# Order of GpSimd's and VectorE's first instructions in a four-layer position-dependent convolution network

## The chip, the cores and the metric

The kernel runs on one core of one Trainium2 chip. The metric is the device time of one execution in microseconds (us), taken as the median over the executions that were timed. A profiled execution is a separate one, and its trace gives start and duration of the instructions of each engine: PE (TensorE matmul, with PEld for its weight loads), DVE (VectorE), ACT (ScalarE), POOL (GpSimd) and SP (SyncE, which here only starts transfers).

## The reference

Four layers, each added to its input: x = x + layer(group_norm(x)), with x of shape (4, 32, 32, 16). Layers 0, 1 and 3 are of one kind, and nearly all of the time goes into them. Cut to what matters:

```
def conv(inputs, M, W, G):            # inputs: batch 4, 32 x 32, 16 channels
    first = einsum('ijyx,byxc->bijc', M, inputs)
    kern = G as (1024*16, 16, 3, 3)   # a 3x3 kernel for each of 1024 output places, 16 channels
    shifted = conv2d(inputs, kern, padding='SAME')       # 16384 images of 32 x 32 for each batch element
    diff = relu(inputs[:, None, None] - shifted)
    second = einsum('ijyx,bijyxc->bijc', W, diff)
    return first - second
```

Layer 2 is a small network of running maxima and 16-wide products; the change does not touch it.

## The kernel before

**Tiling.** The batch of four is done as two groups of two images, and the three large layers times two groups give six phases (`conv_layer`). A phase has 8 chunks of 128 output places. A chunk is 32 steps, one for each of 16 channels f and two images b. A step is one [128 x 1024] result in PSUM (`pc`), made by matmuls over the nine taps (eight taps as two times 64 rows on each half, the ninth on its own), and then one VectorE instruction (line 728, tile `junk`) which takes min(result, 0), multiplies it by the weights `WT` and adds up along the row. There are 1536 steps. The PSUM pool has four buffers of that size, so the first matmul of step k can start when the line 728 instruction of step k-4 has read its buffer.

**Weights and units.** Weights come in units of four channels. Units 0 and 1 of the first chunk (`PLAIN = 2`) are used as they are, in float32: tile `first`, with the ninth tap's weights in `W9`. Their steps are the first 16 and in this order: channels 0 to 3 of image 0, channels 0 to 3 of image 1, then channels 4 to 7 of both in the same way. This text numbers them 0 to 15. Step 16 is the first of unit 2. From unit 2 on, both operands are split into a high and a low part, and the products are taken in a faster format: `ib` and `ia` hold the images' parts in other partitions and `iyz` a difference of parts.

**Preparation of a unit.** From unit 2 on, the generator `prep_parts` prepares units: VectorE cuts off low bits (line 206, tile `upper_w`), ScalarE and GpSimd make `parts` and `W9` (lines 178 and 242 to 251), SyncE copies parts to other partitions (line 257) and loads a later unit (line 111). Ahead of this, GpSimd subtracts one from one tap's weights (`minus_center`, line 220), for unit 2 and later in `raw`, for the plain units in `first`. `prep_plain` and `prep_plain_rest` make a plain unit's `W9` (line 178 on ScalarE, then line 181 on VectorE).

**The first images.** The images of the first phase come by transfer in three slots into `raw`. `sides` sets the edges of the shifted copies (lines 915 and 922), `normal` applies mean and inverse deviation (lines 929, 930 and 932), `halve` and `halve_rest` make the ninth tap's image `im9`.

**Split, place, difference.** For units 2 and later each image is split: `split` has VectorE cut the image (line 206, tile `upper_x`) and subtract (line 289, two instructions, one for each slot s), and ScalarE scale the upper part (line 293). Both write into `temp`, which lies in `first` behind the plain weights. `place` has SyncE copy from `temp` into `ib` (line 305, four transfers) and `ia` (line 311, four transfers). `difference` (line 297, one instruction for each s) makes `iyz` on VectorE from `temp`. A write of the second image's part of `temp` by line 289 waits for two of the first image's `ia` transfers, the second and the fourth, since the ranges that they read reach into it.

**What sets the order.** Each engine runs its instructions in the order in which the program issues them. `conv_layer` issues one step at a time; between steps it takes the next piece of the generators `prep_parts` and `behind`. A `yield 1` of `behind` puts the following piece behind the next step, `yield 2` behind the one after that. In the first phase `behind` runs `rest_of_start` first, where two of the three edits are; the other stands in the straight code before it. In the order of issue, a step's matmuls of its first part come ahead of the line 728 instruction of the step before.

Of the kernel before, what the change touches and what calls it, by code (L numbers as in the profile page):

```python
# [18 lines left out]
GB = B // NG  # L19
# [26 lines left out]
def net_kernel(ctx: ExitStack, tc: tile.TileContext, x, xq, xi, convs, iv_w, iv_b, out):  # L46
# [26 lines left out]
    nc = tc.nc  # L73
# [33 lines left out]
    def load_raw(u):  # L107
        if u < n_chunks * NU:
            n = u // NU
            raws[u] = wpool.tile([P, 3, FU, P], F32, tag="raw", bufs=RAWS, name=f"raw_{u}")  # L110
            nc.sync.dma_start(raws[u], convs[phases[n // NT][1]][2][n % NT, u % NU])
# [65 lines left out]
    def halve(dst, src, mask):  # L177
        nc.scalar.activation(dst, src, AF.Copy, scale=mask[:, 1:2])  # L178

    def halve_rest(dst, src, mask):  # L180
        nc.vector.scalar_tensor_tensor(  # L181
            dst, src, mask[:, 0:1], dst.bitcast(F32), op0=ALU.mult, op1=ALU.add
        )
# [5 lines left out]
    def zeros(g):  # L189

        nc.gpsimd.memset(xt[g], 0.0)
        for y in (0, HP - 1):
            nc.gpsimd.dma_start(
                xs[g][:, :, y * WP : (y + 1) * WP], zero[:GC].rearrange("p (h n) -> p h n", h=2)
            )
# [3 lines left out]
    def image(v, x):  # L199
        return v.rearrange("... (y x) -> ... y x", x=x)[..., :HW]  # L200
# [10 lines left out]
    def prep(u, at=0, to=FU, eng=nc.gpsimd):  # L211

        if u >= n_chunks * NU:
            return
        for s in range(2 if u < PLAIN else 1):
            minus_center(eng, u, s, at, to)

    def minus_center(eng, u, s, at, to):
        f0 = u % NU * FU
        eng.tensor_tensor(  # L220
            raws[u][:, s, at:to], raws[u][:, s, at:to],
            pick[s][:, f0 + at : f0 + to].unsqueeze(2).to_broadcast([P, to - at, P]),
            ALU.subtract,
        )
# [46 lines left out]
    def prep_plain(u, at=0, to=FU, eng=nc.gpsimd):  # L271
        plain_unit(u)
        prep(u, at, to, eng)
        halve(units[u][3][:, at:to], raws[u][:, 2, at:to], low_p)

    def prep_plain_rest(u, at=0, to=FU):
        halve_rest(units[u][3][:, at:to], raws[u][:, 2, at:to], low_p)

    def halves(temp, b):
        v = temp[:, :TEMP].rearrange("p (k s b n) -> p k s b n", k=2, s=2, b=GB)  # L280
        return v[:, 0, :, b], v[:, 1, :, b]

    def split(eng, g, b, temp, name, pause=IDLE):

        ty, tz = halves(temp, b)
        high = upper(image(raw[:, :2, b], WP), 2, f"x{name}{b}")
        yield 1
        for s in range(2):
            eng.tensor_tensor(
                image(tz[:, s], HW), image(raw[:, s, b], WP), image(high[:, s], HW), ALU.subtract  # L290
            )
            yield pause
            nc.scalar.activation(ty[:, s], high[:, s], AF.Copy, scale=EPS)  # L293

    def difference(eng, g, b, s, temp):
        ty, tz = (v.bitcast(F32)[:, s] for v in halves(temp, b))
        eng.tensor_tensor(iyz[g][:, s, b], ty, tz, ALU.subtract)

    def place(g, b, temp):

        parts = halves(temp.bitcast(F32)[:, :TEMP], b)
        da, db = (v[g].bitcast(F32)[:, :, b] for v in (ia, ib))
        for lo, hi in QUARTERS:
            for to, src in zip((lo, hi), parts):
                nc.sync.dma_start(db[to], src[hi])
        for h, (lo, hi) in enumerate(QUARTERS):
            for k, to in enumerate((lo, hi)):
                at = (2 * k * GB + b) * NH + HW * (1 - h)
                pitch = GB * NH + HW * (2 * h - 1)
                src = temp.bitcast(F32)[lo, at : at + 2 * pitch].rearrange("p (s n) -> p s n", s=2)  # L310
                nc.sync.dma_start(da[to, :, :LAST], src[:, :, :LAST])
        yield 1
# [468 lines left out]
    def behind(phase):  # L781
        g, layer = phases[phase]
        if phase == 0:
            yield from rest_of_start()
            nc.sync.dma_start(X[1], x[1])
            zeros(1)
            yield 6
            yield from constants()
        if phase + 1 < len(phases):
            g1, layer1 = phases[phase + 1]  # L790
            if layer1 == 2:
                yield from interval_layer(g1)
            terms = g1 == NG - 1 and layer1 < NL - 1
            yield from before_conv(g1, layer1)
            if terms:
                mt = yield from load_first_terms(layer1)
                yield from first_terms(layer1, mt)
        if phase == len(phases) - 1:
            mt = yield from load_first_terms(layer)
            yield from first_terms(layer, mt)  # L800
            yield 4
            nc.sync.dma_start(out[1 - g], X[1 - g])
# [107 lines left out]
    def sides(eng, b, slot, only=("left", "right", "top", "bottom")):  # L910

        v = raw[:, slot, b].rearrange("p (y x) -> p y x", x=WP)
        if slot == 2:
            at = v[64:, :, HW - 1]
            eng.tensor_scalar(at, at, mean0[64:, b : b + 1], None, op0=ALU.add)
        for side, at in (
            ("left", v[:, :, 0]), ("right", v[:, :, HW - 1]),
            ("top", v[:, 0, :HW]), ("bottom", v[:, H - 1, :HW]),
        ):
            if side in only and f"{side}{slot}" in keep:  # L920
                k = keep[f"{side}{slot}"]
                eng.tensor_scalar(  # L922
                    at, at, kept[:, k : k + 1], fill[:, b, k : k + 1], op0=ALU.mult, op1=ALU.add
                )

    def normal(eng, b, slot):
        v = raw[:, slot, b, :RUN]
        if eng is nc.scalar:
            eng.activation(v, v, AF.Identity, bias=minus_mean0[:, b : b + 1])
            eng.activation(v, v, AF.Copy, scale=rstd0[:, b : b + 1])  # L930
        else:
            eng.tensor_scalar(  # L932
                v, v, mean0[:, b : b + 1], rstd0[:, b : b + 1], op0=ALU.subtract, op1=ALU.mult
            )

    sides(nc.vector, 0, 0)
    sides(nc.gpsimd, 0, 2)
    minus_center(nc.gpsimd, 0, 1, 0, F0)
    sides(nc.gpsimd, 0, 1, ("left", "right"))
    nc.vector.reciprocal(rstd0, rstd0)  # L940
    normal(nc.scalar, 0, 2)
    normal(nc.vector, 0, 0)
# [7 lines left out]
    def rest_of_start():  # L950

        nc.sync.dma_start(X[0], x[0])
        load_raw(2)
        load_raw(3)
        prep_plain_rest(0, F0, FU)
        yield 1
        sides(nc.gpsimd, 1, 2)
        sides(nc.gpsimd, 1, 1, ("left", "right"))
        sides(nc.vector, 1, 0)
        sides(nc.vector, 1, 1, ("top", "bottom"))  # L960
        for eng, slot in ((nc.scalar, 2), (nc.vector, 0), (nc.vector, 1)):
            normal(eng, 1, slot)
        halve(image(im9[0][:, 1], HW), image(raw[:, 2, 1], WP), low_x)
        halve_rest(image(im9[0][:, 1], HW), image(raw[:, 2, 1], WP), low_x)
        prep_plain(1)
        prep(2)
        yield 1
        prep_plain_rest(1)
        yield 1
        temp = first.bitcast(F32R)[:, used:]  # L970
        for b in range(GB):
            yield from split(nc.vector, 0, b, temp, "00", 1)
            yield from place(0, b, temp)
            for s in range(2):
                difference(nc.vector, 0, b, s, temp)
            yield 1
        nc.gpsimd.memset(zero, 0.0)
        nc.vector.memset(part, 0.0)
        zeros(0)
        xns[0] = work.tile([P, NT, GC], F32, tag="xn", bufs=2, name="xn_00")  # L980
        yield from group_norm(0, "c00", xns[0], 4, CALM)
# [83 lines left out]
```

## Time and profile before

| | us |
|---|---|
| median of 3 runs | 2467.36 |
| lowest and highest run | 2466.83, 2468.67 |
| the profiled execution | 2469.47 |
| its span, from first to last instruction | 2467.4 |
| PE busy in the span | 2457.5 |
| DVE busy | 2075.6 |
| POOL busy | 1594.7 |
| PE busy from 0 to 52 us | 47.8 |
| PE busy from 52 to 100 us | 48.0 |
| PE busy from 100 to 400 us | 299.9 |
| PE busy from 400 to 2400 us | 1998.8 |

The last four rows are read from a table of busy time by stretches of the span. PE is busy nearly everywhere behind 52 us. Time in which PE has nothing to do lies ahead of 52 us, where the change is made, and at the very end. The granted TensorE clock is 1.00 in each of these stretches.

### The profile page before, as it was taken

To read this page: it belongs to the slowest core of one execution; us is meant where nothing else is said; L and a number is where in the kernel's file an instruction comes from. 1 tells how busy PE (TensorE), PEld (TensorE's weight loads), DVE (VectorE), ACT (ScalarE), POOL (GpSimd) and SP (SyncE) were. 2 spreads that over 40 slices of the span, in tenths; PEclk is the share of its full clock that TensorE was granted. 3 is DMA by queue.
4 is the path that set the end of the run, shared out by engine and by line. 5 is a ranking of instruction groups with operands and counts; after the bars stand their busy time and mean duration, and the time that the engine had idled before them with its cause. 6 is when DMAs were issued, how large, how long until landed. Compare 5 with 4: busy or idle time off the path is not lost.

```text
span 2467.4 us, 58148 instructions
## 1 busy us (share of the span) xinstructions
PE 2457.5 (100%) x21928; PEld 2056.1 (83%) x21928; DVE 2075.6 (84%) x3631; ACT 1873.6 (76%) x2164; POOL 1594.7 (65%) x1864
## 2 busy tenths in 40 slices
PE   9999999999999999999999999999999999999999
PEld 5888888888888888888888888888889888888887
DVE  9888878888888888878898888888888888788887
ACT  4777777787777778767777777777777787677776
POOL 5767665676666667555576876776777675555552
PEclk9999999999999999999999999999999999999999
DMA  7456654485444467644554454664444476554452
GB/s 202 138 156 162 185 179 137 127 200 141 133 143 135 137 168 186 199 113 137 138 139 131 126 142 136 168 179 137 128 136 136 128 206 179 147 148 137 138 137 55
DMA packets 96906, 366.92 MB, mean 149 GB/s; under 512 B 25712, under 2 KB 30704, under 8 KB 96624
## 3 DMA queue, kind: packets, MB, share of 16 engines
q1 hardware_dynamic: 96064, 362.79, 53.4%
q8 instruction: 172, 2.82, 0.5%
q14 instruction: 110, 0.90, 0.1%
q10 hardware_dynamic: 432, 0.39, 0.1%
q0 software_dynamic: 128, 0.02, 0.0%
HBM read 199.78 MB, written 1.02 MB: 81 GB/s over the span
## 4 chain that ended last, share of the span: by engine, by line
PE 96%; DVE 1%; DMA 1%; ACT 1%; issue 1%; POOL 0%; ACTq 0%; DVEq 0%; POOLq 0%
PE pc L675 95%; PE pf L451 1%; DVE junk L728 1%; DMA raw<-in_g 0%; ACT pc L711 0%; DMA first<-in_g 0%; ACT temp L293 0%; PE ps_l L585 0%; DMA ib<-first 0%; PE ps_r L600 0%; DVE raw L922 0%; DVE im L181 0%; DVE W L181 0%; DVE raw L932 0%; ACT im L178 0%
## 5 line engine op out<-in xcount | busy, mean ns | idle before, releaser
L728 DVE SCALAR_TENSOR_TENSOR junk<-pc,WT 128x1024 f32<-128x1024 f32 x1536 | 1879.3, 1224 | 354.4 <-PE pc L675 295.2
L711 ACT ACTIVATE pc<-pc 128x1024 f32<-128x1024 f32 x1520 | 1532.2, 1008 | 560.5 <-PE pc L675 525.2
L675 PE MATMUL pc<-iyz,parts 64*128 64x512 f32 x6080 | 943.3, 387 | 2.1 <-ACT pc L711 1.6
L675 PE MATMUL pc<-ib,parts 64*128 64x512 f32 x6080 | 945.2, 387 | 0.2
L675 PE MATMUL pc<-ia,parts 64*128 64x496 f32 x6080 | 920.8, 379 | 0.0
L675 PEld LDWEIGHTS pc<-ia,parts 64*128 64x128 f32 x6080 | 578.8, 184 | 111.7
L675 PEld LDWEIGHTS pc<-ib,parts 64*128 64x128 f32 x6080 | 576.9, 184 | 108.4 <-issue 5.0
L675 PEld LDWEIGHTS pc<-iyz,parts 64*128 64x128 f32 x6080 | 577.3, 184 | 97.9 <-ACT pc L711 7.3
L675 PE MATMUL pc<-im,W 64*128 64x496 f32 x3072 | 598.6, 383 | 0.0
L243 POOL TENSOR_TENSOR parts<-raw,upper_w 128x512 fp32r<-128x512 f32 x190 | 249.5, 1313 | 522.7 <-DVE upper_w L206 440.9
L675 PEld LDWEIGHTS pc<-im,W 64*128 64x128 f32 x3072 | 292.7, 184 | 59.9 <-issue 3.3
L249 POOL CAST parts<-parts 32x512 fp32r<-32x512 f32 x380 | 231.7, 610 | 36.0 <-ACT parts L246 17.4
L247 POOL TENSOR_TENSOR parts<-parts 128x512 fp32r<-128x512 f32 x190 | 247.5, 1303 | 1.6 <-ACT parts L242 1.5
L244 POOL TENSOR_TENSOR W<-W,raw 128x512 fp32r<-128x512 f32 x190 | 247.8, 1304 | 0.3 <-ACT W L178 0.3
L251 POOL CAST parts<-upper_w 32x512 fp32r<-32x512 f32 x380 | 233.1, 613 | 22.8
L220 POOL TENSOR_TENSOR raw<-raw,ident 128x512 f32<-128x512 f32 x190 | 197.9, 1042 | 59.3 <-DMA raw<-in_g 35.4
L178 ACT ACTIVATE W<-raw,low_w 128x512 fp32r<-128x512 f32 x190 | 136.2, 717 | 3.7 <-DMA raw<-in_g 3.7
L728 DVE DVE_READ_ACCUMULATOR junk<-pc,WT 128x1 f32 x1536 | 127.6, 83 | 0.0
L242 ACT ACTIVATE parts<-upper_w 128x512 fp32r<-128x512 f32 x190 | 118.7, 624 | 3.8 <-DVE upper_w L206 3.7
L246 ACT CAST parts<-upper_w 128x512 fp32r<-128x512 f32 x190 | 116.1, 611 | 0.0
L743 POOL TENSOR_SCALAR acc<-acc 128x32 f32<-128x32 f32 x40 | 15.7, 392 | 133.9 <-DVE junk L728 132.1
L206 DVE TENSOR_SCALAR upper_w<-raw 128x512 int32<-128x512 int32 x190 | 82.1, 432 | 10.2 <-POOL raw L220 9.9
(158 smaller groups left out, 481.2 us busy)
## 6 DMA issues: line engine op xcount, KB each, us to landing
raw<-in_g SPq DMA_DIRECT2D x190, 768.0 KB, 7.2
parts<-parts SPq DMA_DIRECT2D x380, 384.0 KB, 5.0
WT<-in_w SPq DMA_DIRECT2D x48, 512.0 KB, 4.8
MT<-in_mt SPq DMA_DIRECT2D x24, 512.0 KB, 7.5
raw<-xs SPq DMA_DIRECT2D x120, 71.8 KB, 3.5
ib<-temp SPq DMA_DIRECT2D x40, 128.0 KB, 7.4
ia<-temp SPq DMA_DIRECT2D x40, 124.0 KB, 6.0
ib<-first SPq DMA_DIRECT2D x8, 128.0 KB, 4.0
```

The source lines that it names most:

```text
L178: nc.scalar.activation(dst, src, AF.Copy, scale=mask[:, 1:2])
L220: eng.tensor_tensor(raws[u][:, s, at:to], raws[u][:, s, at:to], pick[s][:, f0 + at : f0 + to].unsqueeze(2).to_broadcast([P, to - at, P]), ...
L242: nc.scalar.activation(WD, high, AF.Copy, scale=-EPS)
L243: nc.gpsimd.tensor_tensor(WL, w8, high, ALU.subtract)
L244: nc.gpsimd.tensor_tensor(W9, W9.bitcast(F32), src[:, 2], ALU.add)
L246: nc.scalar.copy(WU, high)
L247: nc.gpsimd.tensor_tensor(WD, WD.bitcast(F32), WL.bitcast(F32), ALU.add)
L249: nc.gpsimd.tensor_copy(WU[hi], WL[lo].bitcast(F32))
L251: nc.gpsimd.tensor_copy(WL[lo], high[hi])
L675: nc.tensor.matmul(ps[:, h, at : at + n], lhsT=w[r], rhs=v[r] if n == NH else v[r][:, :n], start=first and k == 0, stop=k == len(pairs) - ...
L711: nc.scalar.activation(ps, ps, AF.Copy, scale=1.0 + EPS)
L728: nc.vector.scalar_tensor_tensor(junk, ps.rearrange("p h n -> p (h n)"), 0.0, chunks[n], op0=ALU.min, op1=ALU.mult, accum_out=accs[phase][ ...
```

## The change

```diff
     sides(nc.vector, 0, 0)
     sides(nc.gpsimd, 0, 2)
+    sides(nc.gpsimd, 0, 1, ("left", "right"))
     minus_center(nc.gpsimd, 0, 1, 0, F0)
-    sides(nc.gpsimd, 0, 1, ("left", "right"))
     nc.vector.reciprocal(rstd0, rstd0)
...
         prep_plain(1)
         prep(2)
-        yield 1
+        yield 2
         prep_plain_rest(1)
-        yield 1
         temp = first.bitcast(F32R)[:, used:]
         for b in range(GB):
             yield from split(nc.vector, 0, b, temp, "00", 1)
             yield from place(0, b, temp)
+        for b in range(GB):
             for s in range(2):
                 difference(nc.vector, 0, b, s, temp)
             yield 1
```

No instruction is added or removed; some change places.

- On GpSimd, the two edge instructions (line 922) of slot 1 of image 0 come ahead of the subtraction (line 220) of the second half of unit 0's first two channels.
- On VectorE, the instruction that completes unit 1's `W9` (line 181) stood between the line 728 instructions of steps 1 and 2, ahead of `upper_w` of unit 2 (line 206). It now stands behind the line 728 instruction of step 2, ahead of `upper_x` of image 0. `upper_w` of unit 2 thereby comes directly behind the line 728 instruction of step 1.
- On VectorE, the two line 297 instructions of image 0 stood ahead of image 1's `upper_x` and line 289 instructions. They now stand behind them: between the line 728 instructions of steps 10 and 11, and those of image 1 follow between steps 11 and 12, where they were. Image 1's `upper_x` comes one step earlier than before (ahead of the line 728 instruction of step 7), and so do its two line 289 instructions (ahead of those of steps 8 and 9).
- ScalarE's and SyncE's instructions keep their order, and so do all that follow step 12.

## The prediction

> **What bounds the kernel now.** I read the chain that ended last for the whole span, then only its first 100 us in order of time, then the timelines of PE, DVE, POOL and SP there, and the transfers' landings. Over the span PE is the chain:
>
> ```profile
> PE 96%; DVE 1%; DMA 1%; ACT 1%; issue 1%; POOL 0%; ACTq 0%; DVEq 0%; POOLq 0%
> ```
>
> Behind 52 us PE idles 1.7 us in all, so what PE loses or gains ahead of that goes to the end one for one. Ahead of it DVE sets PE's pace. DVE's timeline (start, us; line; what), with the lines that matter:
>
> ```profile
> 19.34 1.53 DVE L181 SCALAR_TENSOR_TENSOR W<-first,low_p,W 128x512 fp32r<-128x512 f32 x1
> 20.79 0.41 DVE L206 TENSOR_SCALAR upper_w<-raw 128x512 int32<-128x512 int32 x1
> 21.13 1.21 DVE L728 SCALAR_TENSOR_TENSOR junk<-pc,WT 128x1024 f32<-128x1024 f32 x1
> ...
> 22.27 0.84 DVE L206 TENSOR_SCALAR upper_x<-raw 128x1024 int32<-128x1024 int32 x1
> 23.03 1.21 DVE L728 SCALAR_TENSOR_TENSOR junk<-pc,WT 128x1024 f32<-128x1024 f32 x1
> ...
> 28.99 2.13 DVE L297 TENSOR_TENSOR iyz<-first 128x512 fp32r<-128x512 f32 x2
> 31.05 1.21 DVE L728 SCALAR_TENSOR_TENSOR junk<-pc,WT 128x1024 f32<-128x1024 f32 x1
> ...
> 33.94 0.68 DVE L289 TENSOR_TENSOR first<-raw,upper_x 128x512 fp32r<-128x512 f32 x1
> ...
> 39.09 1.35 DVE L297 TENSOR_TENSOR iyz<-first 128x512 fp32r<-128x512 f32 x2
> ```
>
> It has no gap worth naming from 9.9 to 52 us. PE follows it through the four PSUM buffers: step 6 starts at 22.40, when step 2's line 728 (21.13 + 1.21 = 22.34) is done, and step 17 at 43.27, when that of step 13 (42.00 to 43.22) is.
>
> ```profile
> 22.40 1.99 PE L675 MATMUL pc<-raw,first 64*128 64x512 f32 x8 [0.63 <-DVE junk L728]
> ```
>
> GpSimd's timeline:
>
> ```profile
> 16.67 1.06 POOL L220 TENSOR_TENSOR first<-first,ident 128x512 f32<-128x512 f32 x1 [0.16 <-DMA first<-in_g]
> 19.28 1.04 POOL L220 TENSOR_TENSOR raw<-raw,ident 128x512 f32<-128x512 f32 x1 [1.55 <-DMA raw<-in_g]
> 21.28 1.28 POOL L243 TENSOR_TENSOR parts<-raw,upper_w 128x512 fp32r<-128x512 f32 x1 [0.96 <-DVE upper_w L206]
> ...
> 29.15 1.43 POOL L220 TENSOR_TENSOR raw<-raw,ident 128x512 f32<-128x512 f32 x1
> ...
> 39.67 1.28 POOL L193 DMA_DIRECT2D xs<-zero  x2
> 40.93 1.32 POOL L247 TENSOR_TENSOR parts<-parts 128x512 fp32r<-128x512 f32 x1
> ```
>
> Beside DVE's lines these show a shared resource. Line 297 alone takes 0.68; the second of the pair at 28.99 took 1.53 and ended at 31.13, 0.55 behind GpSimd's subtraction (29.15 + 1.43 = 30.58). W at 19.34 ended 0.55 behind 20.32, `upper_x` at 22.27 ended 0.55 behind GpSimd's 22.56. GpSimd waits in turn: that subtraction takes 1.04 alone, and here it ended 0.90 behind the first line 297 (29.68). It got its turn between two adjoining DVE instructions. Line 728 (1.21 to 1.23 throughout) is not held up. My rule from these rows: a DVE instruction of lines 181, 206, 289 or 297 ends 0.55 behind a running GpSimd array instruction, GpSimd ends its duration less 0.15 behind a running DVE one, and they take turns.
>
> Transfers out of the split of image 0:
>
> ```profile
> 24.84 3.70 SPq L305 DMA_DIRECT2D ib<-first  x4
> 28.59 2.53 SPq L311 DMA_DIRECT2D ia<-first  x4
> ```
>
> The second `ib` goes out at 26.62, when the second line 289 is done (26.60); the fourth `ia` at 30.51, 3.89 later, and it lands after 2.3, at 32.81.
>
> **Edit 1, edges ahead of the subtraction.** Slot 1 of image 0 was issued at 2.17 and took 5.9, so the edges cannot start before 8.07; they started at 8.53. So 0.44 is gained for VectorE's edges and line 932 (9.87 to 9.43), and PE's first step ends that much sooner. The subtraction is late instead: 8.9 to about 9.8, ahead of PE's need at about 10.1. The gain does not last. Image 1's fifth edge instruction on DVE (14.65) needs GpSimd's edges, which end at 14.52 by a transfer that landed at 13.1; 0.10 is left. Then `im` (line 181, 16.75) runs behind GpSimd's 16.67 subtraction and ends at 18.27 as before, so step 1's line 728 starts at 18.20 as before. Cost 0. Should `im` slip in ahead of that subtraction, step 1 is 0.9 sooner, and edit 2's wait takes that back.
>
> **Edit 2, W one step later.** `upper_w` now comes at 19.34 and needs GpSimd's subtraction in `raw`, which ends at 20.32. W covered this wait; now DVE idles to 20.36, **+1.02**. Line 728 of step 2 then runs 20.70 to 21.91, PE's step 6 starts at 21.97 (0.43 sooner). W comes at 21.84 while GpSimd's line 243 runs (20.85 to 22.13) and ends at 22.68; line 244, in waiting, takes its turn (to 22.68 + 1.28 - 0.15 = 23.81); `upper_x`, from 22.60, ends at 24.36. W and `upper_x` take 0.76 + 1.68 = 2.44 against 1.45 + 0.76 = 2.21 before: **+0.23**. Step 3's line 728 starts at 24.28 instead of 23.03, so PE's step 7 starts at 25.55 instead of 24.45, and idles 1.5 ahead of it. W's reader, step 8, comes past 27 us.
>
> **Edit 3, differences behind both splits.** Line 728 of steps 4 to 6 keeps its distance; that of step 6 starts at 29.08 (27.84 before). Then `upper_x` of image 1 (0.61) and step 7 (1.14), and DVE stands at line 289 of image 1 at 31.97. This waits for the fourth `ia`. Image 0's second line 289 ends at 27.84, the second `ib` goes at 27.86, the fourth `ia` at 31.75, and it lands at 34.05. Before, the two line 297 (2.06) and step 8 stood ahead and covered it; now DVE idles to 34.08, **+2.11**, with steps 8 to 12 of line 728 queued behind, and PE behind those. From there: step 8 at 34.68, step 9 at 36.42, `upper_w` 37.56, step 10 at 37.90, line 297 of image 0 at 39.04. GpSimd's lines 243 and 244 start from that `upper_w`, and one step less lies between: line 243 (38.05 to 39.33) holds the first line 297 to 39.88, line 244 takes its turn to 41.01, the second ends at 41.56. Step 11 at 41.48; image 1's line 297 at 42.62. GpSimd's line 247 comes 1.64 behind the end of line 244 (before: 39.29 to 40.93), at 42.65. So the first goes just ahead (to 43.30), line 247 then runs to 44.45, the second ends at 45.00. The two pairs take 2.44 + 2.30 against 2.06 + 1.28: **+1.40**. One pause of 0.18 between two adjoining line 728 (37.77 to 37.95) goes: **-0.18**. The pairs' readers are far off: step 16's second part.
>
> **The sum** is 1.02 + 0.23 + 2.11 + 1.40 - 0.18 = 4.58. Step 12's line 728 starts at 44.92 against 40.37, so PE's step 17 waits for step 13 until 47.8 instead of 43.27. From step 13 to 52 us DVE's order is the same, and PE's last gap there (0.48 at 51.40, behind ScalarE, which waited for `upper_w` at 49.34) moves along. Nothing later gives it back, PE being full. Against the profiled execution (2469.47; span 2467.4, 2.1 above the median) this is 2474.05; on the median, 2467.36 + 4.6 = **2472.0**.
>
> **Bounds.** Of the terms, the landing is measured. The turns are an inference from three pairs: if DVE's next instruction went first instead, `upper_x` would save 1.1 and the pairs 2.1, and 1.4 is left. If line 247 beat image 1's first line 297 (0.03 apart), that would end at 44.5, wait again for line 249, and the pair end 0.5 later: 5.1.
>
> The rule that speaks for worse is the Trainium skill's "TensorE: Matmul & The Clock Gate", section "Part 1: The HAM clock gate": after an idle window of some 3.4 us PE falls to half its clock. The trace has a granted clock of 1.00 across PE's gap of 1.25 us at 9.3. The gaps worked out here are at most 1.5, so by the rule it costs nothing as well; if a window did count, an estimate from that page's figure is 1.7 us more. No run here shows it.
>
> **Rivals.**
> - *Line 247 first* (0.30): +5.1, 2472.5. For it: 0.03 us between two sums of rounded rows. Against: DVE is the earlier one by these rows. This ends on the slower side, since 0.2% (about what a measurement of this kernel can tell from no change) is 4.93 us, 2472.3. It decides if line 297 of image 1 starts 0.03 later.
> - *Landing late* (0.10): the unit load behind the `ia` transfers overlaps them. Image 1's `ib` and `ia`, which ran beside such a load, took 4.7 to 8.4. With 4.7 for the fourth it is +2.4, 2474.4. Against: SP issues the load behind the fourth.
> - *DVE goes first* (0.17): +1.4, to 3.5 if only one of the places goes so: 2468.8 to 2470.9.
> - *The change does what its words suggest* (0.05): PE keeps the 0.43 of step 6 and DVE's new waits are covered by something I overlook; PE's gaps before 52 us that could go (step 0 takes 8.17 to 11.89, 1.78 more than the 1.94 of a later one; then 0.63, 0.2, 0.48) bound the gain to 3.1, so it stays within 0.2%; 2466.
>
> **How the numbers follow.** My forecast has 0.36, own range 2471.5 to 2472.6; the 0.02 left over goes to faster by something unseen. A third of the forecast's chance lies over 2472.3. Slower: 0.30 + 0.10 + 0.12 = 0.52. Same: 0.24 + 0.17 + 0.05 = 0.46. Range 2469.2 to 2473.6: outside lie the late landing, the gain and about a third of the third rival, 0.2.
>
> **What would show it.** In the changed trace: DVE idle of about 1.0 ahead of `upper_w` near 20.4, released by GpSimd's line 220; `upper_x` of 1.7 or more; idle of about 2 ahead of line 289 near 34, released by a transfer; the pairs of line 297 near 2.4 each; PE at step 17 near 47.8; the same gaps as before past 53. It is wrong if line 289 does not wait, if the pairs take 1.3, or if PE at step 17 is ahead of 46.

## The result: slower by 0.24%, and the profile after

| | us |
|---|---|
| kernel before, median of 11 runs | 2467.61 (2466.83 to 2469.02) |
| changed kernel, median of 11 runs | 2473.30 (2472.36 to 2475.66) |
| difference | +5.7 |
| ratio, with its 95% interval | 1.0024 [1.0015, 1.0033] |
| profiled execution of the changed kernel | 2472.92, its span 2470.8 |

The interval has no 1 in it: the change costs time, between 3.7 and 8.1 us, and 5.7 is just over the 0.2% (4.93 us) that the prediction drew as its line. The forecast of 2472.0 was 1.3 short.

DVE's timeline of the changed kernel (start and duration in us, engine, line, operation; in brackets an idle time and what ended it):

```profile
19.63 0.43 DVE L206 TENSOR_SCALAR upper_w<-raw 128x512 int32<-128x512 int32 x1 [0.22 <-POOL raw L220]
...
21.11 0.85 DVE L181 SCALAR_TENSOR_TENSOR W<-first,low_p,W 128x512 fp32r<-128x512 f32 x1
21.88 1.75 DVE L206 TENSOR_SCALAR upper_x<-raw 128x1024 int32<-128x1024 int32 x1
23.56 1.21 DVE L728 SCALAR_TENSOR_TENSOR junk<-pc,WT 128x1024 f32<-128x1024 f32 x1
...
33.50 0.69 DVE L289 TENSOR_TENSOR first<-raw,upper_x 128x512 fp32r<-128x512 f32 x1 [2.14 <-DMA ia<-first]
...
38.48 2.53 DVE L297 TENSOR_TENSOR iyz<-first 128x512 fp32r<-128x512 f32 x2
40.93 1.21 DVE L728 SCALAR_TENSOR_TENSOR junk<-pc,WT 128x1024 f32<-128x1024 f32 x1
...
42.07 2.91 DVE L297 TENSOR_TENSOR iyz<-first 128x512 fp32r<-128x512 f32 x2
44.90 1.21 DVE L728 SCALAR_TENSOR_TENSOR junk<-pc,WT 128x1024 f32<-128x1024 f32 x1
```

Three things are new in it: an idle of 2.14 us ahead of line 289 of image 1, a short wait ahead of `upper_w`, and pairs of line 297 that hold DVE for 2.45 (38.48 to 40.93) and 2.83 (42.07 to 44.90), where they held it 2.06 and 1.28 before. The last row is step 12's line 728: 44.90, against 40.37 before and 44.92 in the prediction's sum.

What the idle waits for is in the chain of waits of the changed kernel, cut to these moments (start, duration, what):

```profile
29.11 0.60 SPq L311
29.76 0.60 SPq L311
30.40 0.59 SPq L311
31.04 2.33 DMA ia<-first
33.40 0.05 DVEq L289
33.50 0.06 DVE first L289
```

The fourth `ia` transfer goes out at 31.04, takes 2.33, and line 289 starts when it has landed. GpSimd's timeline shows what the pairs run beside:

```profile
37.49 1.28 POOL L243 TENSOR_TENSOR parts<-raw,upper_w 128x512 fp32r<-128x512 f32 x1 [8.10 <-DVE upper_w L206]
38.73 1.73 POOL L244 TENSOR_TENSOR W<-W,raw 128x512 fp32r<-128x512 f32 x1
...
42.09 1.31 POOL L247 TENSOR_TENSOR parts<-parts 128x512 fp32r<-128x512 f32 x1
43.47 1.98 POOL L249 CAST parts<-parts 32x512 fp32r<-32x512 f32 x2
```

Image 0's pair meets lines 243 and 244; image 1's pair (42.07) meets line 247 (42.09), which takes its undisturbed 1.31 and so went first, and then line 249, of which the two take 1.98 together. PE's timeline then shows the bill:

```profile
42.20 1.99 PE L675 MATMUL pc<-raw,first 64*128 64x512 f32 x8 [0.72 <-DVE junk L728]
43.62 0.79 PE L675 MATMUL pc<-im,W 64*128 64x496 f32 x2
46.22 1.25 PE L675 MATMUL pc<-ib,parts 64*128 64x512 f32 x4 [1.81 <-POOL parts L251]
46.98 1.31 PE L675 MATMUL pc<-ia,parts 64*128 64x496 f32 x4
47.81 1.34 PE L675 MATMUL pc<-ib,parts 64*128 64x512 f32 x4
48.83 1.15 PE L675 MATMUL pc<-ia,parts 64*128 64x496 f32 x4
49.66 0.80 PE L675 MATMUL pc<-iyz,parts 64*128 64x512 f32 x4
```

The row at 46.22 is step 16's first, with 1.81 us of nothing ahead of it. The releaser named there, a line 251 of GpSimd, belongs to the next unit; by time it was DVE, whose step 12 ended at 44.90 + 1.21 = 46.11. Step 17 starts at 47.81 (43.27 before). From there the four `ib` and four `ia` matmuls take 1.85, to 49.66; in the kernel before they took 1.07 (43.27 to 44.34). The windows of the changed kernel say why (window, its length, busy time of PE, PEld, DVE, ACT and POOL with their instructions; then the granted clock, the DMA share and GB/s):

```profile
47.00:48.00 1.00, 1.00 (x8) 0.79 (x6) 0.90 (x3) 0.00 (x0) 0.90 (x1) 0.50 0.11 25
48.00:49.00 1.00, 1.00 (x8) 1.00 (x8) 1.00 (x1) 0.67 (x1) 0.00 (x0) 0.50 1.12 240
...
50.00:51.00 1.00, 1.00 (x12) 1.00 (x11) 0.65 (x3) 0.99 (x1) 0.00 (x0) 1.00 1.01 289
```

By the trace's record of the clock it was half from 46.48 to 49.90, for 3.41 us, and full on both sides. The kernel before has 1.00 in all of this stretch. Six steps on, PE's step 22 starts at 57.16 against 52.19: +4.97 in this pair of executions. Behind that PE is full: it is busy 339.90 of the 340 us from 60 to 400 (339.91 before) and 499.91 of the 500 from 400 to 900 (499.91 before). That the two spans differ by 3.4 only is chance of the profiled execution of before, which was 1.9 above its median and lost 0.8 between 900 and 1400 us (499.13 busy, against 499.91).

### The profile page after: what moved, and what is told of

It reads as the page before. It is cut to its first block, busy times and chain, and to the rows that moved or that the text cites. A ratio compares the mean times of both kernels' runs of the same rounds, so it can differ in the third digit from the quotient of the medians.

```text
span 2470.8 us, 58149 instructions
## 1 busy us (share of the span) xinstructions
PE 2460.2 (100%) x21928; PEld 2068.0 (84%) x21928; DVE 2077.0 (84%) x3631; ACT 1873.4 (76%) x2164; POOL 1595.3 (65%) x1864
## 3 DMA queue, kind: packets, MB, share of 16 engines
HBM read 199.78 MB, written 1.02 MB: 81 GB/s over the span
## 4 chain that ended last, share of the span: by engine, by line
PE 97%; DMA 1%; ACT 1%; issue 1%; DVE 0%; POOL 0%; SPq 0%; ACTq 0%; DVEq 0%; POOLq 0%
PE pc L675 96%; PE pf L451 1%; DMA first<-in_g 0%; ACT pc L711 0%; DMA raw<-in_g 0%; DVE junk L728 0%; ACT temp L293 0%; PE ps_l L585 0%; DMA ia<-first 0%; PE ps_r L600 0%; POOL parts L249 0%; SPq L305 0%; SPq L311 0%; DVE upper_x L206 0%; POOL W L244 0%
## 5 line engine op out<-in xcount | busy, mean ns | idle before, releaser
L249 POOL CAST parts<-parts 32x512 fp32r<-32x512 f32 x380 | 232.3, 611 | 36.7 <-ACT parts L246 18.2
```

What stands on the lines that cost most here:

```text
L249: nc.gpsimd.tensor_copy(WU[hi], WL[lo].bitcast(F32))
```

## The experiments

All times are medians of 10 or 11 runs (5 for the one kernel that lost 17 us), set against the kernel before on the same chip. The intervals are about 2 us to each side, so single differences under 2 us are not told apart by the times alone, and the profiles carry those.

**Each edit by itself.** The first kernel has only the two lines of edit 1 exchanged.

```diff
+    sides(nc.gpsimd, 0, 1, ("left", "right"))
     minus_center(nc.gpsimd, 0, 1, 0, F0)
-    sides(nc.gpsimd, 0, 1, ("left", "right"))
```

> The kernel before with the first edit alone (GpSimd's edges of slot 1 ahead of its subtraction). My theory: step 0 on PE ends about 0.4 us sooner, and VectorE loses this lead at image 1's edges and at the line 181 that stands behind GpSimd's subtraction, so the time is that of before, 2467.6 within 0.4, with step 1's line 728 at 18.2 as before. Rival (the lead lasts, since PE starts sooner): 0.4 to 0.5 faster, 2467.1, and step 17 on PE about 0.4 sooner.

Measured: 2468.64 against 2468.52, ratio 1.0001 [0.9993, 1.0010]. No effect. In its profile GpSimd's edges ran from 8.09 beside VectorE's line 932 and took 1.10 instead of 0.78, and PE's first matmuls were not sooner. Step 1's line 728 came at 19.59 and not at the expected 18.2: in this execution two of VectorE's edge instructions of image 1 took 1.1 each beside GpSimd's line 220, where the others took 0.3.

The second has only the `yield 2` of edit 2:

```diff
-        yield 1
+        yield 2
         prep_plain_rest(1)
-        yield 1
```

> The kernel before with the second edit alone (unit 1's W9 on VectorE one step later). My theory: VectorE waits up to 1.0 us ahead of upper_w for GpSimd's subtraction, upper_x takes about 1.7 instead of 0.8, and step 3's line 728 is about 1.2 late; then image 0's line 297 pair no longer meets GpSimd's subtraction and takes 1.3 instead of 2.1, which gives 0.8 back. Step 17 on PE is 0.3 to 0.5 late: 2468.0. Rival A (this edit makes most of the loss): over 3 us, 2470.6 or more. Rival B (PE's step 6 keeps its 0.4 to 0.6): 2467.0.

Measured: 2469.45, +0.9, ratio 1.0003 [0.9994, 1.0011]: within the noise. DVE's timeline in it:

```profile
19.31 0.43 DVE L206 TENSOR_SCALAR upper_w<-raw 128x512 int32<-128x512 int32 x1
...
20.80 0.86 DVE L181 SCALAR_TENSOR_TENSOR W<-first,low_p,W 128x512 fp32r<-128x512 f32 x1
21.58 1.75 DVE L206 TENSOR_SCALAR upper_x<-raw 128x1024 int32<-128x1024 int32 x1
```

Here `upper_w` didn't wait at all: GpSimd's line 220 was done. W and `upper_x` behaved as foretold (0.78 and 1.67 by their starts). Image 0's line 297 pair, which no longer met GpSimd's subtraction, took 1.29 instead of 2.13, as expected, and with that step 12's line 728 came at 39.76, not later than the 40.37 before.

The third has only edit 3:

```diff
             yield from place(0, b, temp)
+        for b in range(GB):
             for s in range(2):
```

> The kernel before with the third edit alone (both images' differences behind both splits). My theory: VectorE waits about 2.0 us at image 1's first line 289 for the fourth ia transfer, and each line 297 pair takes 2.3 to 2.9 instead of 2.1 and 1.3; step 17 on PE is 3.3 late, and if PE's gap ahead of step 16 is again 1.8 us and its clock falls to half for 3.4 us, as in the changed kernel, about 0.8 more: 2470.9 to 2471.7. Rival (the three edits only cost together, each alone is covered): within 1 us of before.

Measured: 2472.66, +4.1, ratio 1.0015 [1.0006, 1.0024]. PE's gap of 1.81 is there again, and the clock is 0.83 over 42 to 52 us. Its DVE timeline shows the wait and both long pairs:

```profile
32.08 0.69 DVE L289 TENSOR_TENSOR first<-raw,upper_x 128x512 fp32r<-128x512 f32 x1 [2.04 <-DMA ia<-first]
...
37.06 2.54 DVE L297 TENSOR_TENSOR iyz<-first 128x512 fp32r<-128x512 f32 x2
...
40.66 2.91 DVE L297 TENSOR_TENSOR iyz<-first 128x512 fp32r<-128x512 f32 x2
```

Edit 3 has the loss. The next kernels take it apart.

**The changed kernel without the wait.** The two images' parts of `temp` are interleaved, and the range that image 0's `ia` transfers read, from its first to its last element, reaches into the range of image 1; no element is in both. Here the images lie one behind the other, so that the ranges are apart as well. Nothing else differs; lines behind 270 move up by 1 to 4.

```diff
-        v = temp[:, :TEMP].rearrange("p (k s b n) -> p k s b n", k=2, s=2, b=GB)
+        order = "p (b k s n)" if apart else "p (k s b n)"
+        v = temp[:, :TEMP].rearrange(order + " -> p k s b n", k=2, s=2, b=GB)
...
+                if apart:
+                    at = (2 * GB * b + 2 * k) * NH + HW * (1 - h)
+                    pitch = NH + HW * (2 * h - 1)
```

> The changed kernel with each image's parts of temp in a range of their own, so that line 289 of image 1 need not wait for image 0's ia transfers; the same instructions otherwise (in this file the lines behind 270 have numbers higher by 1 to 4). My theory: the 2.1 us of idle ahead of line 289 go, the long line 297 pairs stay (2.4 and more each), PE's gap ahead of step 16 falls under 1 us and the granted clock stays at 1.00: 2.1 to 3.0 faster than the changed kernel, about 2470.6. Rival A (the wait was covered by PE's own work): 2473 as the changed kernel. Rival B (the pairs are long because of the wait's timing): 4 or more faster, 2469 or less.

Measured: 2471.86, +3.3, ratio 1.0015 [1.0006, 1.0023]. Its DVE timeline (line 290 is the old 289, 298 the old 297):

```profile
31.37 0.69 DVE L290 TENSOR_TENSOR first<-raw,upper_x 128x512 fp32r<-128x512 f32 x1
...
36.34 2.54 DVE L298 TENSOR_TENSOR iyz<-first 128x512 fp32r<-128x512 f32 x2
...
39.94 2.91 DVE L298 TENSOR_TENSOR iyz<-first 128x512 fp32r<-128x512 f32 x2
```

And its PE timeline (line 679 is the old 675):

```profile
44.09 0.82 PE L679 MATMUL pc<-ib,parts 64*128 64x512 f32 x4 [1.40 <-POOL parts L251]
```

The idle is gone and the pairs are as long as before. PE's gap is 1.40, longer than the 1 us that was expected at most, and the clock stays at 1.00. So the wait of 2.1 us was one on a range and not on data.

**The changed kernel with image 0's pair a step sooner.** The pair goes ahead of unit 3's `upper_w`, which starts GpSimd's lines 243 and 244; the wait stays.

```diff
-            yield from place(0, b, temp)
+            yield from place(0, b, temp, pause=1 - b)
...
-            yield 1
+            yield 2 - b
```

> The changed kernel with image 0's line 297 pair one step sooner, ahead of unit 3's upper_w, which releases GpSimd's lines 243 and 244, and image 1's pair where it was; image 1's line 289 still waits for the ia transfers. My theory (the pairs are long because they run beside GpSimd): each pair takes 1.3 instead of 2.5 and 2.9, VectorE is 2.7 sooner at step 12, PE's gap ahead of step 16 falls under 1 us and its clock stays at 1.00: 2.7 to 3.5 faster than the changed kernel, 2.2 to 3.0 slower than before. Rival A (the wait for the ia transfers makes all of the loss, and the pairs' time is hidden): still 4.5 or more slower than before. Rival B (a pair is long wherever both stand behind the splits, by the data's place): the pairs still take 2.4 or more.

Measured: 2470.22, +2.3, ratio 1.0010 [1.0001, 1.0019]; clock 1.00. DVE's timeline:

```profile
33.18 0.69 DVE L289 TENSOR_TENSOR first<-raw,upper_x 128x512 fp32r<-128x512 f32 x1 [2.11 <-DMA ia<-first]
...
36.68 1.29 DVE L297 TENSOR_TENSOR iyz<-first 128x512 fp32r<-128x512 f32 x2
...
40.70 1.35 DVE L297 TENSOR_TENSOR iyz<-first 128x512 fp32r<-128x512 f32 x2
```

The same instructions on the same data take half as long: GpSimd's line 247 now starts at 42.53, behind both pairs.

**Neither wait nor long pairs**: both edits above together.

> The changed kernel with both: each image's parts of temp in a range of their own, so that line 289 does not wait for the ia transfers, and image 0's line 297 pair ahead of unit 3's upper_w. My theory (wait, pairs and the clock are the whole loss but for what edit 2 makes): within 1 us of before, 0 to 0.9 slower, pairs of 1.3, no idle ahead of line 289, granted clock 1.00 throughout. Rival (something else in the third edit costs): 2 us or more slower than before.

Measured: 2468.03, +0.1, ratio 1.0002 [0.9993, 1.0011]; the pairs take 1.29 and 1.35, line 290 doesn't wait, the clock is 1.00. With that the loss is split:

| | pairs beside GpSimd | pairs alone |
|---|---|---|
| wait on the range | +5.7 (the changed kernel; again: +6.3) | +2.3 |
| no wait | +3.3 | +0.1 |

The two causes add up (3.3 + 2.3 = 5.6), closer than times with some 2 us to either side can show: the medians alone tell the corners apart (5.7 or 6.3 against 0.1), and that each cause goes with its edit is read from the profiles. The price of the clock's fall is in the corner with both causes. What is left of edits 1 and 2 is not measurable.

**Does the mended third edit bring something?** The kernel before, with edit 3, the images apart and the pairs sooner, but without edits 1 and 2.

> The kernel before with the third edit in the form of the last run (ranges of their own, image 0's pair ahead of unit 3's upper_w), and neither of the other two edits. My theory: image 0's pair takes 1.3 instead of 2.1, VectorE is 0.8 sooner from step 7 on, and PE's short gaps at steps 11 and 17 go: 0.3 to 0.8 faster than before. Rival (PE is not held there): same as before within 0.2.

Measured: 2467.85, -0.1, ratio 1.0000 [0.9991, 1.0008]. A miss, or too small to see: nothing gained.

**The same with edit 2 and every prepared unit one step later**, so that neither W nor `upper_w` stands between the line 728 instructions of steps 1 and 2. Image 1's pair comes one step later too, to stay clear of GpSimd's lines 243 and 244:

```diff
-    FIRST = 3
+    FIRST = 4
...
-            yield 2 - b
+            yield 3 - 2 * b
```

> As the last run, and with the second edit, and with prep_parts started one step later (FIRST = 4), so that neither W nor upper_w stands between the line 728 instructions of steps 1 and 2, and image 1's pair one more step later to stay clear of GpSimd's lines 243 and 244. My theory: step 2's line 728 follows step 1's at once, PE's gap of 0.6 to 0.8 at step 6 goes as well, and no line 728 is held by GpSimd's subtraction: 0.8 to 1.6 faster than before. Rival (the work that is put off only makes the gap at step 7 instead): same as before within 0.3.

Measured: 2485.45, +17.5, ratio 1.0069 [1.0056, 1.0082]. A clear miss. PE is busy for all of 22 to 42 us in it, so the start was as wanted; the loss is later. The largest of PE's waits in it (engine, line and releaser: us in all, times, longest):

```profile
PE pc L680 <- DMA parts<-parts: 7.3, 8, 2.1
```

And a window of the same kernel, with columns as above:

```profile
400.00:1000.00 600.00, 590.97 (x5226) 497.26 (x5226) 492.79 (x854) 456.05 (x524) 378.68 (x447) 1.00 0.56 149
```

PE is idle for 9 us of 600 in this stretch, where the kernel before is busy 599.03. In the whole run it waits eight times for parts that SyncE copies (line 257), 7.3 us in all, and four times for VectorE's line 733 (the old 728), 4.3 us. A step of later preparation for each unit used up a reserve that a few units need. To see that it is this, and not the start, the next kernel makes only unit 2 late, catches up at step 9, and has image 1's pair where it was:

```diff
-                if n == 0 and at in (20, 24):
+                if n == 0 and at in (9, 20, 24):
```

> Run e7's kernel with the second edit and with unit 2's preparation alone started one step later and caught up by step 9, so that the units behind keep their steps. My theory: what cost 17 us in run e8 was that every later unit came one step later, and PE then waited for its transfers; with that mended, step 2's line 728 follows step 1's at once, and the time is 0.2 to 0.8 under e7's, 2467.2 to 2467.7. Rival (the start itself made e8 slow): 2475 or more.

Measured: 2468.62, +0.6, ratio 1.0004 [0.9995, 1.0013]. The 17 us are gone, so the later units had cost them; and no gain is to be measured here either. No version beat the kernel before.

**The changed kernel again, and the clock.** The fall of the clock was not in the prediction's sum, so the changed kernel was run again, beside the version without the wait that has its gap lengthened: two instructions whose result nobody reads (0.86 us for both) ahead of step 12's line 728.

```diff
+            if b == 1:
+                for _ in range(2):
+                    nc.vector.tensor_reduce(
+                        part[:, : GC // 2], X[0].rearrange("p t (g s) -> p g t s", s=2),
+                        axis=AX.XY, op=ALU.add,
+                    )
```

> The changed kernel once more, beside the next run on the same chip, to have its gap ahead of step 16, its clock and its pairs in a second execution. My theory: 5 to 6 slower than before, a gap of about 1.8 us ahead of step 16, the granted clock at half for 3.4 us from there, image 1's pair 2.9 because GpSimd's line 247 goes ahead of it. Rival (the clock's fall was a chance of one execution): clock 1.00 here.

> The kernel of run e4 (no wait for the ia transfers; gap of 1.4 us ahead of step 16, clock at 1.00) with two idle sums on VectorE (0.4 us each, of a kind that GpSimd's work does not hold) ahead of step 12's line 728, so that PE's gap grows to some 2.0 to 2.2 us, while nothing else is added. My theory (a gap of that length there halves the clock for 3.4 us, and this costs 0.8 besides the gap): the clock falls as in the changed kernel, and the time is 1.4 to 1.7 over e4's, 4.5 to 5.0 slower than before. Rival (the clock does not fall, or its fall costs nothing): 0.7 over e4's, 4.0 slower than before.

Measured: the changed kernel 2474.31, +6.3, ratio 1.0023 [1.0013, 1.0032]; the lengthened one 2472.03, +4.0, ratio 1.0018 [1.0009, 1.0027]. PE's timeline of the lengthened one:

```profile
44.94 0.82 PE L679 MATMUL pc<-ib,parts 64*128 64x512 f32 x4 [2.17 <-POOL parts L251]
...
46.53 1.22 PE L679 MATMUL pc<-ib,parts 64*128 64x512 f32 x4 [0.31 <-DVE junk L732]
47.55 1.03 PE L679 MATMUL pc<-ia,parts 64*128 64x496 f32 x4
48.37 1.05 PE L679 MATMUL pc<-iyz,parts 64*128 64x512 f32 x4
```

With a gap of 2.17 the clock fell in a kernel that kept it at 1.40: half for 3.41 us, from 46.55. It came a step later than in the first profile of the changed kernel; the same holds for the second (gap 1.81 at 47.91, slow matmuls from 49.50). That the longer gap brings the fall is shown for this pair of kernels; the last section has what decides it over all profiles. What it costs is not settled by the times: +0.7 over the version with the short gap is what the rival without a price for the fall expected. PE's rows say more than that. The eight matmuls from 46.53 on take 1.84 here, and 1.02 in the version with the short gap (45.68 to 46.70); from 59 us on, where both are past it, the lengthened one stands 1.82 behind, of which 0.85 is the longer gap itself. Between steps 19 and 21 it was 2.43 behind; the rest came back because PE, being late, did not wait for ScalarE, as it does for 0.64 in the version with the short gap. But the profiled execution with the short gap lost 1.3 later on, in one wait, and both spans are 2470.7. So the fall cost some 1 us in PE's rows, which the medians do not confirm.

## Why the prediction was right, step by step

| step of the sum | predicted | profile of the changed kernel |
|---|---|---|
| edit 1 | 0 | step 1's line 728 at 18.18 (18.20 before) |
| `upper_w` waits for line 220 | +1.02 | +0.30 (19.33 to 19.63) |
| W and `upper_x` | +0.23 | 0.77 + 1.68 against 2.21: +0.24 |
| line 289 waits for the landing | +2.11 | 31.27 to 33.50: +2.23 |
| the two pairs | +1.40 | 2.45 + 2.83 against 3.34: +1.94 |
| pause between two line 728 | -0.18 | gone |
| step 12's line 728 | 44.92 | 44.90 |
| half clock behind PE's gap | 0 | +0.78 |
| gap of before at 51.40 moves along | 0 | about -0.4 |
| PE at step 22 | +4.58 | +4.97 |

**Edit 3's wait** was right in place and cause, and in size within 0.12. The two kernels without it confirm it: no idle in their profiles, and times of 5.7 to 3.3 where the pairs stay long, 2.3 to 0.1 where they don't.

**The pairs** were right in cause. The term was mis-sized by 0.54, at the one place that the prediction had called a near tie: it put image 1's first line 297 just ahead of GpSimd's line 247, and line 247 went first in all five profiles with long pairs, although the pair's start is 0.02 the earlier in each. The rival *Line 247 first* priced that at +0.5, and it is what happened, so of the prediction's own cases it is this one that came true, not the forecast. Its 2472.5 is nearer to 2473.3.

**Edit 2's wait** was over-sized. The term took GpSimd's line 220 to end at 20.32 as in the one execution shown. It starts when unit 2's load lands, and that moved: it started at 19.28 there and at 18.55 in the changed kernel, where 0.30 was left. In the six experiments' profiles with `upper_w` in that place, DVE idles ahead of it once, for 0.37, and five times not at all. Near nothing is the better price, and what edit 2 costs by itself, +0.9, can't be told from zero.

**Edit 1** was right at nothing, but not for the reason given. The prediction had VectorE's line 932 and PE's first step 0.44 sooner, and let this lead be lost at image 1's fifth edge instruction. In the profile there was no lead to lose: line 932 starts at 9.88 (9.87 before) and step 1 on PE at 11.91 (11.89). GpSimd's edges, now beside another line 932 of VectorE, take 1.07 in the changed kernel, 1.10 with edit 1 alone and 1.04 in the changed kernel's second profile, instead of 0.78, and VectorE's two edges take 0.76 instead of 0.49.

**The clock** was priced at nothing because "the gaps worked out here are at most 1.5". The gap was 1.81, since the pairs were longer, and the clock fell. The Trainium skill's "TensorE: Matmul & The Clock Gate", section "Part 1: The HAM clock gate", was weighed there as asking for an idle window of 3.4 us. The traces differ from that reading: the fall came with 1.81 us of idle, PE being busy for 47% of the 3.41 us ahead of it. The page's length of a window, 3413 ns, is the length of each fall. Its estimate in the prediction, 1.7 us if a window counted, bounds what the rows show, +0.78 in the first profile, where 1.33 of the 3.41 us at half clock lay ahead of step 17, which waited for DVE anyway. About 0.4 of the 0.78 came back by step 22: PE, being late, hardly waited at the gap that the kernel before has at 51.40.

So the mechanism was right in edit 3, and the total was near for a mixture of reasons: one term was 0.7 too large, two were too small, by 0.5 and 0.1, and one, the clock, was missing. That step 12's line 728 came within 0.02 of the sum is luck, these errors having cancelled. That the medians differ by 5.7 and the profile's step 22 by 5.0 is inside the interval of 3.7 to 8.1, and no run tells where the rest is.

## What to carry to other kernels

Before moving an instruction later, ask what it covered: the pair of line 297 had stood in front of a landing 2.1 us away, and the dependency behind that landing was only one of address ranges, which another layout removed. Moving an instruction also changes what runs beside it: the same two subtractions took 1.3 or 2.9 us, depending on whether GpSimd's were running. Neither mended form gained anything, and shifting all later preparation by one step to make room cost 17 us: what looks like slack at the start can be the reserve of a few units later on.

## What the hardware showed that was not expected

- **The clock falls without a long pause.** Gaps of PE of 1.81, 1.81, 1.81 and 2.17 us, in otherwise busy stretches, were each followed by 3.41 us at half clock, and so was one of 2.09 in the kernel with later units (it ends at 914.09, the fall begins at 914.90). The gap of 1.40 was not, nor was the kernel before's 1.25 at 9.3. The fall begins 0.26 to 1.65 us behind the gap's end.
- **What orders these cases is the busy share of a stretch on a fixed grid.** In all 13 profiles the changes of the clock lie whole multiples of 3.413 us apart: 37.547 us is 11 of them, 40.960 is 12, 2420.050 is 709. The five falls above came at the end of stretches of this grid in which PE was busy for 47, 47, 38, 38 and 38% (43.07 to 46.48 in the changed kernel: 1.60 of 3.41 us), and those at the kernels' ends after 33% or less. The lowest shares without a fall are 57 and 59%, both in the kernel without the wait (the 59% has the gap of 1.40). So the limit lies between 47 and 57% here, and a gap counts by how much of it falls into one stretch.
- **VectorE and GpSimd in turns.** Where they meet, the lag of the prediction's rule comes back: line 297's pair ends at 41.01, 0.55 behind line 244 (38.73 + 1.73 = 40.46). The Trainium skill's "SBUF — State Buffer", section "Who interferes with whom", says that a VectorE instruction with two SBUF inputs contends with a GpSimd instruction that reads SBUF, that the lock is exclusive, and that the order of issue decides which of the two is blocked. The rows agree: line 297, with two inputs there, is held; line 728, one of whose inputs is in PSUM, takes 1.19 to 1.23 in all its 1536 instructions; and line 247 takes its full 1.31 while line 297 waits. Which of these two is first can't be read from their starts: line 297's is the earlier one, by 0.02. Line 206, with a single SBUF input, is held too: `upper_x` takes 1.75 beside GpSimd's line 244 and 0.69 without it (at 29.52).
